# Loading x two groups ahead, counting in a sequence of its own and spreading the offset stores in a four-layer convolution kernel

## The chip, the cores and the metric

The kernel runs on one core of a Trainium2 chip. The metric is the device time of one execution in microseconds (us). A core has five engines that run side by side and wait for each other through semaphores: TensorE (PE; its weight loads are shown apart as PEld), VectorE (DVE), ScalarE (ACT), GpSimd (POOL) and SyncE (SP). SP issues nearly all DMAs of this kernel.

## The reference, cut to what matters

Four layers are applied to `x`, an array of 4 x 128 x 128 x 128 floats (batch, channel or row, row or column, column), each as `x = x + layer(group_norm(x))`. The change lies in the first, a deformable 3x3 convolution with a rectifier:

```python
offset = jnp.einsum('bchw,oc->bohw', x, w_off) + b_off[None, :, None, None]
# py, px: the position of each tap plus its offset; (y0, x0) its floor
val = gather(y0i, x0i) * (wy0 * wx0)[:, :, None]
...
return jnp.einsum('bgckhw,ogck->bohw', val, wg)      # wg: w_def by groups
...
x = x + _L0_conv_ref(_gn(x), L0_conv_w_off, L0_conv_b_off, L0_conv_w_def)
```

For each of 9 taps and 4 groups of channels every pixel has an offset of its own, and the value there is interpolated from four neighbours. The group normalization `_gn` takes its statistics over 4 neighbouring columns, all rows and all of axis 1, in each batch, so they must be known before the batch's offsets can be computed. The other layers are a scan along rows with a 9-tap convolution, a message layer, and a triangle multiplication with gates. They are the same before and after.

## The kernel before, in words

`deform_layer` (line 182) computes the first layer. It doesn't gather. It lays a table of normalized pixels out in DRAM (`tabs`), with 32 windows of 4 columns plus their margins along each row, and stores the offsets in DRAM (`offs`), in three bf16 parts that add up to a float. A batch is cut into 43 blocks of 3 output rows; with 4 batches there are 172. For a block the offsets come back as `places`, the table as `pixels`. TensorE spreads the offsets of a tap over 120 lanes (`spread_offsets`, line 459, into `t_ps`, two buffers), ScalarE makes the distance and a tent of it (`tents`, 471), VectorE the second tent's negative and VectorE or GpSimd, in turn, the product (`product`, 478). `sample` (484) multiplies the pixels with the products, `keep_samples` (498) copies the samples out of PSUM (`v_ps`, two buffers), and `convolved` (540) makes the convolution, with `finish` (516) adding `x` and storing.

The order of instructions on all five engines is written out by hand: each engine executes them in the order in which the program emits them. The main loop (line 652) has eight units per block, one for each group of four windows. In a unit, spreading runs two units ahead, tents one unit ahead, and products are made for the coming block. At the end of a unit `step` is called once, or twice while fewer than 26 rows are ready beyond the block.

`step` (583) advances a generator to its next `yield`. This is the work beside the main loop, one generator at a time: `counted` (326), the statistics of a whole batch from 1 MB loads, four steps of eight statistics instructions for each of the 8 loads and then the normalization; `prepared` (359), which prepares a chunk of 16 rows; or `x1_norm`, for the layer's result. The loads of `counted` and `prepared` share one buffer, `xin`. A chunk in `prepared` has 32 steps: the load of 16 rows (line 364), then for each of 4 groups of 4 rows seven steps: transposes (371), the normalized `rows` on ScalarE with the stores to the table after every second group (374 to 381), the matmul of the offsets (386), their scale and shift, and three steps that split them into `parts` (ScalarE's copy, line 405, with VectorE's running maximum and minimum and GpSimd's subtraction). Last come 18 stores from `parts` to `offs` (line 419), six to a step, and the end. `parts` is one buffer for a chunk of 16 rows.

SP's queue is in order too. At the start of each block it takes the four loads of `places` for the block after next, the four of `pixels` for the next block, and one of the residual `xres`; the loads and stores of `prepared` come between them where they were emitted. `need` (603) makes the steps that a load of `places` requires, if they were not made yet.

Of the kernel before, what the change touches and what calls it, by code (L numbers as in the profile page):

```python
# [2 lines left out]

# [6 lines left out]
F32 = mybir.dt.float32  # L10
# [3 lines left out]
ALU = mybir.AluOpType  # L14
# [4 lines left out]
P = 128  # L19
# [162 lines left out]
def deform_layer(tc, c, small, x, w_off, b_off, w_def, x1, tabs, offs):  # L182
# [13 lines left out]
    with ExitStack() as ctx:  # L196
# [126 lines left out]

        scales = {}

        def counted(b, dense):

            stats = one.tile([P, NGN, S // RC, 6], F32, name="stats0")
            for r in range(S // RC):
                if dense:  # L330
                    xc = three.tile([P, RC, S], F32, name="xc", tag="v")
                else:
                    xc = one.tile([P, RC, S], F32, name="xin")
                nc.sync.dma_start(xc, x[b, :, r * RC : (r + 1) * RC, :])
                yield
                for g in range(NGN):
                    nc.vector.bn_stats(stats[:, g, r, :], xc[:, :, g * GS : (g + 1) * GS])
                    if g % 8 == 7:
                        yield
            got = []  # L340
            yield from gn_steps(nc, c, one, keep, ps_g, stats, "x", got)
            _, s, t = got
            across = ps_g.tile([2 * NL, 2, P], F32, name="st_ps", tag="gn_ps")
            for i, v in enumerate((s, t)):
                diag = one.tile([P, P], F32, name=f"diag_{i}")
                nc.vector.tensor_scalar(diag, c.ident, v, None, ALU.mult)
                nc.tensor.matmul(
                    across[:, i], lhsT=c.ones[:, 0 : 2 * NL], rhs=diag, start=True, stop=True
                )
            yield  # L350
            st = keep.tile([2 * NL, 2, P], F32, name="st")
            nc.vector.tensor_copy(st, across)

            koff = keep.tile([2 * NL, S], F32, name="koff")
            nc.vector.tensor_scalar(koff, st[:, 1], wsum, boff, ALU.mult, ALU.add)
            scales[b] = (s, t, st, koff)
            yield

        def prepared(b, y0):

            s, t, st, koff = scales[b]
            table = tabs[b].rearrange("x (r s) c -> x r s c", s=SX)
            xc = one.tile([P, RC, S], F32, name="xin")
            nc.sync.dma_start(xc, x[b, :, y0 : y0 + RC, :])
            yield
            for h in range(0, RC, RO):
                if h % (2 * RO) == 0:
                    rows = one.tile([P, 2 * RO, P], F32, name="rows")
                pt = ps_g.tile([P, RO, P], F32, name="img_ps", tag="gn_ps")
                for i in range(RO):  # L370
                    nc.tensor.transpose(pt[:, i], xc[:, h + i, :], c.ident)  # L371
# [12 lines left out]
                yield  # L384
                po = ps_g.tile([2 * NL, RO, S], F32, name="off_ps", tag="gn_ps")
                nc.tensor.matmul(po, lhsT=woff, rhs=xc[:, h : h + RO, :], start=True, stop=True)
# [9 lines left out]
                n = (b * S + y0 + h) // RO  # L396
                flat = off.rearrange("p r c -> p (r c)")

                rest = one.tile([2 * NL, RO, S], F32, name="rest")
                left = off  # L400
                for i in range(NSPLIT):
                    part = parts[:, i, h * OW : (h + RO) * OW].rearrange(
                        "p (r c) -> p r c", c=OW
                    )[:, :, 2 : S + 2]
                    nc.scalar.copy(part, left)
                    if i < 2:
                        nc.vector.tensor_reduce(
                            ranges[:, i, n : n + 1], flat, AX.X, (ALU.max, ALU.min)[i]
                        )
                    if i + 1 < NSPLIT:  # L410
                        nc.gpsimd.tensor_tensor(rest, left, part, ALU.subtract)
                        left = rest
                    yield
            for k in range(NK):
                ky, kx = k // 3 - 1, k % 3 - 1
                r0 = (y0 + ky + 1) * OW
                for d in range(2):
                    p0 = d * NL + k * NG
                    nc.sync.dma_start(
                        offs[b][d, k % 2, :, k // 2, r0 : r0 + RC * OW].rearrange(  # L420
                            "(n g) c -> g n c", g=NG
                        ),
                        parts[p0 : p0 + NG, :, 1 - kx : 1 - kx + RC * OW],
                    )
                if k % 3 == 2 and k + 1 < NK:
                    yield

        def load_places(b, j):
            t = places[(b * NYB + j) % 3]
# [39 lines left out]
            return tp, n  # L469

        def tents(tp, n):
            dist = two.tile([LANES, 2, NB], F32, name="dist")
            nc.scalar.activation(dist[:, :, 0:n], tp[0:LANES, :, 0:n], AF.Abs)  # L473
            tent = two.tile([LANES, NB], F32, name="tent")
            nc.scalar.activation(tent[:, 0:n], dist[:, 0, 0:n], AF.Relu, bias=1.0, scale=-1.0)  # L475
            return dist, tent, n

        def product(m, dist, tent, n, engine):

            neg = two.tile([LANES, NB], F32, name="neg")  # L480
            nc.vector.tensor_scalar(neg[:, 0:n], dist[:, 1, 0:n], 1.0, 1.0, ALU.min, ALU.subtract)  # L481
            engine.tensor_tensor(m, neg[:, 0:n], tent[:, 0:n], ALU.mult)  # L482

        def sample(m, pix, i, rows):

# [86 lines left out]
        beside = {"now": None, "norms": [], "count": 1}  # L572
# [6 lines left out]
        def rows_of(b, y0):  # L579
            yield from prepared(b, y0)  # L580
            ready[b] = y0 + RC

        def step(b, row):

            if beside["now"] is None:
                nb = next((i for i in range(b, B) if ready[i] < S), B)
                lead = (nb - b) * S + (ready[nb] if nb < B else 0) - row
                if beside["norms"]:
                    beside["now"] = beside["norms"].pop(0)
                elif beside["count"] <= min(nb, B - 1) or (lead > 20 and beside["count"] == b + 1 < B):  # L590
                    beside["now"] = counted(beside["count"], False)
                    beside["count"] += 1
                elif nb < B:
                    beside["now"] = rows_of(nb, ready[nb])
                else:
                    return False
            try:
                next(beside["now"])
            except StopIteration:
                beside["now"] = None  # L600
            return True

        def need(b, row):
            while ready[b] <= min(row, S - 1):
                step(b, row)

# [35 lines left out]
        for _ in counted(0, True):  # L642
            pass
        load_row(0)
        load_row(1)
# [6 lines left out]
        for n, (b, j) in enumerate(blocks):  # L652
# [11 lines left out]
            for i in range(NG_X):  # L664
# [8 lines left out]
                if end and i < 6:  # L673
# [4 lines left out]
                    else:  # L678
                        product(me[:, kx, :], *tents(*ends[kx]), nc.vector)
                count(6)  # L680
                for _ in range(2 if ready[b] < min(S, RY * j + 26) else 1):
                    step(b, RY * j + 2)
            for _ in convs:
                pass
            if j == 0:
# [22 lines left out]
            pass  # L708
        count(len(to_count))
        beside["norms"].append(x1_norm(B - 1, stats))  # L710
        while step(B, S):
            pass


# [671 lines left out]
```

## Time and profile before

| what | us |
|---|---|
| runs before: lowest, median, highest | 8644.56, 8714.38, 8768.25 |
| the profiled execution | 8805.67 |
| its span, first to last instruction | 8803.9 |
| first sampling matmul (line 491) | 245.7 |
| last copy of samples (line 507) | 4455.9 |
| busy in the span: PE, DVE, ACT, POOL | 7117.6, 5000.0, 3346.5, 1721.0 |

The profile is one execution; the profiled one took 91 us more than the median. Its page gives busy times by engine, 40 slices of the span (about 220 us each), and groups of instructions by line, with the name of the tile written, an arrow, and the tiles read. "Idle before" is the time an engine stood before an instruction, and the releaser is what ended that. A line of the timeline has start, duration, engine, line, operation and, in brackets, the idle time before it; like instructions in a row are merged. SPq is SP's DMA queue: its times are those of issuing a DMA, not of moving the data. The deformable layer lies in the first 20 slices.

### The profile page before, as it was taken

What the parts mean: (1) busy time and instruction counts of PE and PEld (TensorE: products, weight loads), DVE (VectorE), ACT (ScalarE), POOL (GpSimd) and SP (SyncE); (2) the same over time, 40 slices, a digit from 0 to 9 for tenths busy, and PEclk for the clock granted to TensorE, in tenths of its full rate; (3) what the DMA queues carried; (4) which work ended last, traced back from release to release, by engine and by line L of the source; (5) the groups of instructions that cost most, each with busy time, mean ns of one, the idle gap of its engine ahead of it and who ended that gap; (6) DMA issues with size and microseconds to landing.
All of it is one profiled execution on the core that took longest, in us unless ns stands there. A gap on an engine that the chain in (4) does not pass through costs nothing. (4 is left out here: it accounts for less than half of the span.)

```text
span 8803.9 us, 105220 instructions
## 1 busy us (share of the span) xinstructions
PE 7117.6 (81%) x35800; PEld 5835.4 (66%) x35800; DVE 5000.0 (57%) x13104; ACT 3346.5 (38%) x5404; POOL 1721.0 (20%) x1791
## 2 busy tenths in 40 slices
PE   0668777978789777799989999698679668966986
PEld 0556565756567556677778888398549647963985
DVE  5545555755557555577744444447626752674466
ACT  0445554555555555466621111122312312231223
POOL 0123222233222223222200000112112120212121
PEclk9778887988878888799999999688759876976897
DMA  2333333433333333343321221100100010001000
GB/s 66 88 67 77 76 74 69 98 76 80 73 72 98 72 74 76 68 80 61 64 65 60 67 67 54 53 1 10 42 25 1 20 58 1 1 29 48 1 10 29
DMA packets 978744, 473.48 MB, mean 54 GB/s; under 512 B 705076, under 2 KB 931988, under 8 KB 963860
## 3 DMA queue, kind: packets, MB, share of 16 engines
q1 hardware_dynamic: 951216, 428.93, 20.3%
q10 hardware_dynamic: 26980, 37.73, 1.2%
q8 instruction: 284, 4.65, 0.2%
q14 instruction: 264, 2.16, 0.1%
HBM read 284.15 MB, written 182.35 MB: 53 GB/s over the span
## 5 line engine op out<-in xcount | busy, mean ns | idle before, releaser
L491 PEld LDWEIGHTS v_ps<-m,pixels 120*128 120x128 f32 x11008 | 1512.9, 206 | 221.5 <-issue 69.3
L473 ACT ACTIVATE dist<-t_ps 120x780 f32<-120x780 f32 x1560 | 1266.5, 812 | 983.6 <-DVE neg L481 848.5
L491 PE MATMUL v_ps<-m,pixels 120*128 120x108 f32 (+1 forms) x11008 | 1610.0, 291 | 20.1 <-DVE v L502 14.9
L502 DVE COPY v<-v_ps 128x432 f32<-128x432 f32 x1376 | 809.6, 588 | 1390.4 <-PE v_ps L491 1386.9
L551 PE MATMUL conv_ps<-v,wneg 128*128 128x128 f32 (+2 forms) x5160 | 1382.6, 403 | 14.8 <-DVE v L507 14.8
L482 POOL TENSOR_TENSOR m<-neg,tent 120x390 f32<-120x390 f32 x688 | 700.9, 1019 | 2785.1 <-DVE neg L481 2508.1
L551 PEld LDWEIGHTS conv_ps<-v,wneg 128*128 128x128 f32 x5160 | 851.6, 205 | 305.5 <-issue 181.6
L1029 PE MATMUL conv_ps<-carry,wconv 128*128 128x256 f32 x4572 | 1009.5, 378 | 0.3 <-issue 0.3
L1029 PEld LDWEIGHTS conv_ps<-carry,wconv 128*128 128x128 f32 x4572 | 850.8, 188 | 121.3 <-issue 0.6
L475 ACT ACTIVATE tent<-dist 120x390 f32<-120x390 f32 x1560 | 823.0, 528 | 213.7 <-POOL m L482 155.9
L1226 PE MATMUL proj_ps<-wcat,X 128*128 128x128 f32 x4096 | 903.0, 384 | 0.0
L1226 PEld LDWEIGHTS proj_ps<-wcat,X 128*128 128x128 f32 x4096 | 901.5, 313 | 0.0
L1231 DVE SCALAR_TENSOR_TENSOR work<-proj_ps,rstd,pbias 128x128 f32<-128x128 f32 x2048 | 613.2, 344 | 293.3 <-issue 173.7
L464 PE MATMUL t_ps<-places,spread 14*120 14x390 bf16 x3096 | 581.4, 388 | 214.2 <-ACT dist L473 166.1
L482 DVE TENSOR_TENSOR m<-neg,tent 120x390 f32<-120x390 f32 x860 | 652.1, 758 | 91.1 <-DVE neg L481 1.4
L481 DVE TENSOR_SCALAR neg<-dist 120x390 f32<-120x390 f32 x1560 | 630.9, 414 | 42.2 <-ACT dist L473 41.2
L464 PEld LDWEIGHTS <-spread 14*120 14x120 bf16 x3120 | 221.8, 129 | 515.8 <-issue 414.8
L1011 ACT ACTIVATE rowT<-x1T_ps,t_x,s_x 128x128 f32<-128x128 f32 x512 | 192.4, 458 | 862.7 <-PE x1T_ps L1007 417.2
L371 PE MATMUL img_ps<-ident,xin 128*128 128x128 f32 x512 | 98.1, 325 | 514.4 <-DMA xin<-in_x_dram 511.5
L1240 POOL TENSOR_TENSOR right<-work,sig 128x128 f32<-128x128 f32 x512 | 240.6, 471 | 1362.4 <-ACT sig L1236 1138.0
L1303 PE MATMUL gT_ps<-ident,cen 128*128 128x128 f32 x512 | 124.0, 424 | 468.5 <-DVE cen L1298 412.1
L1236 ACT ACTIVATE sig<-work 128x256 f32<-128x256 f32 x512 | 213.4, 417 | 639.1 <-DVE work L1231 639.1
(185 smaller groups left out, 8134.4 us busy)
## 6 DMA issues: line engine op xcount, KB each, us to landing
pixels<-tab SPq DMA_DIRECT2D x688, 120.0 KB
xin<-in_x_dram SPq DMA_DIRECT2D x56, 1024.0 KB
tab<-rows SPq DMA_DIRECT2D x384, 128.0 KB
x<-x1c SPq DMA_DIRECT2D x32, 1024.0 KB
x1rows<-x SPq DMA_DIRECT2D x128, 256.0 KB
x2T<-x2c ACTq DMA_DIRECT2D x128, 256.0 KB
X<-x2T SPq DMA_DIRECT2D x16, 2048.0 KB
out_dram<-res SPq DMA_DIRECT2D x64, 512.0 KB
```

The lines of the kernel that those rows point to most:

```text
L464: nc.tensor.matmul(tp[0:LANES, d, 0:n].rearrange("p (r c) -> p r c", c=PADW), lhsT=spread[p0 : p0 + 14, :], rhs=src[p0 : p0 + 14, k, :, 0: ...
L473: nc.scalar.activation(dist[:, :, 0:n], tp[0:LANES, :, 0:n], AF.Abs)
L475: nc.scalar.activation(tent[:, 0:n], dist[:, 0, 0:n], AF.Relu, bias=1.0, scale=-1.0)
L481: nc.vector.tensor_scalar(neg[:, 0:n], dist[:, 1, 0:n], 1.0, 1.0, ALU.min, ALU.subtract)
L482: engine.tensor_tensor(m, neg[:, 0:n], tent[:, 0:n], ALU.mult)
L491: nc.tensor.matmul(vp[:, h * n : h * n + rows * w].rearrange("p (k c) -> p k c", c=w), lhsT=pix[0:LANES, xb, :], rhs=m[:, :, RX * xb : RX ...
L502: nc.vector.tensor_copy(v[:, :, c0 : c0 + full * RX].rearrange("p k (h c) -> p k h c", c=RX), vp[:, 0 : full * n].rearrange("p (h k c) -> ...
L551: nc.tensor.matmul(pc[:, at : at + r1 - r0, :], lhsT=wneg[:, 3 * ky + kx, :], rhs=v[:, k0 + kx, r0:r1, kx : kx + S], start=m == 0, stop=m ...
L1029: nc.tensor.matmul(pc, lhsT=wt[:, k, :], rhs=old[h][:, :, k : k + S], start=(k == 0), stop=(k == TAPS - 1),)
L1226: nc.tensor.matmul(pp[:, j], lhsT=X[:, :, j0 + j], rhs=wcat[:, cols], start=True, stop=True)
L1231: nc.vector.scalar_tensor_tensor(pre[:, j], pp[:, j], rstd[:, j0 + j : j0 + j + 1], pbias[:, cols], ALU.mult, ALU.add,)
L1240: nc.gpsimd.tensor_tensor(right[:, j0 : j0 + 4, :], pre[:, :, DQ : 2 * DQ], sig[:, :, DQ:], ALU.mult)
```

## The change

It has four parts, all in `deform_layer`.

1. `prepared` takes its rows in loads of 4 rows (256 KB) into three buffers instead of 16 rows into one, and `load_group` issues the loads of the next two groups with each group. The first three are loaded before the first batch is counted. The step that held the load is gone.
2. The statistics of the next batch are no longer one of the generators of `step`. `count_of` loads half rows (16 rows of 64 columns, 512 KB) into a buffer of its own, and the main loop advances it once per unit, from the second unit of a batch on, beside `step`. Each half row takes four units of waiting for the load and two with eight statistics instructions each. After it, `scales_of` is put in line for `step`. Batch 0 is counted at once ahead of the loop.
3. The 18 stores of a chunk's offsets are put on a list when the chunk is done. Three are emitted in each unit, and what is left is emitted in the first group of the next chunk, just ahead of the copies that write `parts` again. A chunk counts as ready when its last store has been emitted. A chunk is now 28 steps and an end.
4. `tents` and `product` keep distance, tent and negative in one tile with three buffers, overwritten in place, instead of three tiles with two buffers each.

The core of the diff:

```diff
-        def counted(b, dense):
+        def count_of(b, stats):
             for r in range(S // RC):
...
+                for h in range(2):
+                    xc = one.tile([P, RC, S // 2], F32, name="xhalf")
+                    nc.sync.dma_start(
+                        xc, x[b, :, r * RC : (r + 1) * RC, h * S // 2 : (h + 1) * S // 2]
+                    )
+                    for _ in range(4):
+                        yield
+                    for g in range(NGN // 2):
+                        nc.vector.bn_stats(
+                            stats[:, h * NGN // 2 + g, r, :], xc[:, :, g * GS : (g + 1) * GS]
+                        )
+                        if g % 8 == 7:
+                            yield
...
+        def load_group(n):
+            if n not in loaded and n < B * S // RO:
+                b, y = n * RO // S, n * RO % S
+                loaded[n] = three.tile([P, RO, S], F32, name="xin")
+                nc.sync.dma_start(loaded[n], x[b, :, y : y + RO, :])
+
+        def store(n):
+            for _ in range(min(n, len(to_store))):
+                to_store.pop(0)()
...
         def prepared(b, y0):
...
-            xc = one.tile([P, RC, S], F32, name="xin")
-            nc.sync.dma_start(xc, x[b, :, y0 : y0 + RC, :])
-            yield
             for h in range(0, RC, RO):
+                n = (b * S + y0 + h) // RO
+                load_group(n)
+                load_group(n + 1)
+                load_group(n + 2)
+                xc = loaded.pop(n)
...
                 yield
+                if h == 0:
+                    store(len(to_store))
                 flat = off.rearrange("p r c -> p (r c)")
...
-            for k in range(NK):
...
-                for d in range(2):
-                    p0 = d * NL + k * NG
-                    nc.sync.dma_start(
...
-                if k % 3 == 2 and k + 1 < NK:
-                    yield
+            def store_tap(k, d):
...
+                nc.sync.dma_start(
...
+                if (k, d) == (NK - 1, 1):
+                    ready[b] = y0 + RC
+            to_store.extend(partial(store_tap, k, d) for k in range(NK) for d in range(2))
...
         def tents(tp, n):
-            dist = two.tile([LANES, 2, NB], F32, name="dist")
-            nc.scalar.activation(dist[:, :, 0:n], tp[0:LANES, :, 0:n], AF.Abs)
-            tent = two.tile([LANES, NB], F32, name="tent")
-            nc.scalar.activation(tent[:, 0:n], dist[:, 0, 0:n], AF.Relu, bias=1.0, scale=-1.0)
-            return dist, tent, n
+            d = three.tile([LANES, 2, NB], F32, name="dist")
+            nc.scalar.activation(d[:, :, 0:n], tp[0:LANES, :, 0:n], AF.Abs)
+            nc.scalar.activation(d[:, 0, 0:n], d[:, 0, 0:n], AF.Relu, bias=1.0, scale=-1.0)
+            return d, n
...
                 count(6)
+                store(3)
                 for _ in range(2 if ready[b] < min(S, RY * j + 26) else 1):
-                    step(b, RY * j + 2)
+                    step()
+                if not (j == 0 and i == 0):
+                    next(beside["count"], None)
+                elif b + 1 < B:
+                    beside["count"] = counting(b + 1)
```

More of the change, by code (lines that the diff above doesn't have):

```diff
@@ L1 @@
 from contextlib import ExitStack
+from functools import partial
 from itertools import chain
@@ L324, in deform_layer, with count_at_once, scales_of @@
         scales = {}
-        def counted(b, dense):
-            stats = one.tile([P, NGN, S // RC, 6], F32, name="stats0")
+        def count_of(b, stats):
             for r in range(S // RC):
-                if dense:
-                    xc = three.tile([P, RC, S], F32, name="xc", tag="v")
-                else:
-                    xc = one.tile([P, RC, S], F32, name="xin")
+                for h in range(2):
[11 more added lines that the diff above has]
+                            yield
+        def count_at_once(b, stats):
+            for r in range(S // RC):
+                xc = three.tile([P, RC, S], F32, name="xc", tag="v")
                 nc.sync.dma_start(xc, x[b, :, r * RC : (r + 1) * RC, :])
-                yield
                 for g in range(NGN):
                     nc.vector.bn_stats(stats[:, g, r, :], xc[:, :, g * GS : (g + 1) * GS])
-                    if g % 8 == 7:
-                        yield
+        def scales_of(b, stats):
             got = []
@@ L357, in counted @@
             yield
+        loaded = {}
+        to_store = []
+        def load_group(n):
[6 more added lines that the diff above has]
+                to_store.pop(0)()
         def prepared(b, y0):
@@ L362, in prepared @@
             table = tabs[b].rearrange("x (r s) c -> x r s c", s=SX)
-            xc = one.tile([P, RC, S], F32, name="xin")
-            nc.sync.dma_start(xc, x[b, :, y0 : y0 + RC, :])
-            yield
             for h in range(0, RC, RO):
+                n = (b * S + y0 + h) // RO
[3 more added lines that the diff above has]
+                xc = loaded.pop(n)
                 if h % (2 * RO) == 0:
@@ L370, in prepared @@
                 for i in range(RO):
-                    nc.tensor.transpose(pt[:, i], xc[:, h + i, :], c.ident)
+                    nc.tensor.transpose(pt[:, i], xc[:, i, :], c.ident)
                 yield
@@ L385, in prepared @@
                 po = ps_g.tile([2 * NL, RO, S], F32, name="off_ps", tag="gn_ps")
-                nc.tensor.matmul(po, lhsT=woff, rhs=xc[:, h : h + RO, :], start=True, stop=True)
+                nc.tensor.matmul(po, lhsT=woff, rhs=xc, start=True, stop=True)
                 yield
@@ L395, in prepared @@
                 yield
-                n = (b * S + y0 + h) // RO
+                if h == 0:
+                    store(len(to_store))
                 flat = off.rearrange("p r c -> p (r c)")
@@ L413, in prepared @@
                     yield
-            for k in range(NK):
+            def store_tap(k, d):
                 ky, kx = k // 3 - 1, k % 3 - 1
                 r0 = (y0 + ky + 1) * OW
-                for d in range(2):
-                    p0 = d * NL + k * NG
[L419 to L424, printed above, removed]
-                if k % 3 == 2 and k + 1 < NK:
-                    yield
+                p0 = d * NL + k * NG
+                nc.sync.dma_start(
+                    offs[b][d, k % 2, :, k // 2, r0 : r0 + RC * OW].rearrange(
+                        "(n g) c -> g n c", g=NG
+                    ),
+                    parts[p0 : p0 + NG, :, 1 - kx : 1 - kx + RC * OW],
+                )
+                if (k, d) == (NK - 1, 1):
+                    ready[b] = y0 + RC
+            to_store.extend(partial(store_tap, k, d) for k in range(NK) for d in range(2))
         def load_places(b, j):
@@ L471, in tents, with product @@
         def tents(tp, n):
-            dist = two.tile([LANES, 2, NB], F32, name="dist")
-            nc.scalar.activation(dist[:, :, 0:n], tp[0:LANES, :, 0:n], AF.Abs)
-            tent = two.tile([LANES, NB], F32, name="tent")
-            nc.scalar.activation(tent[:, 0:n], dist[:, 0, 0:n], AF.Relu, bias=1.0, scale=-1.0)
-            return dist, tent, n
[L478 to L482, printed above, removed]
+            d = three.tile([LANES, 2, NB], F32, name="dist")
+            nc.scalar.activation(d[:, :, 0:n], tp[0:LANES, :, 0:n], AF.Abs)
+            nc.scalar.activation(d[:, 0, 0:n], d[:, 0, 0:n], AF.Relu, bias=1.0, scale=-1.0)
+            return d, n
+        def product(m, d, n, engine):
+            nc.vector.tensor_scalar(
+                d[:, 1, 0:n], d[:, 1, 0:n], 1.0, 1.0, ALU.min, ALU.subtract
+            )
+            engine.tensor_tensor(m, d[:, 1, 0:n], d[:, 0, 0:n], ALU.mult)
         def sample(m, pix, i, rows):
@@ L571, in deform_layer @@
         ready = [0] * B
-        beside = {"now": None, "norms": [], "count": 1}
+        beside = {"now": None, "norms": [], "rows": 0, "count": iter(())}
         def x1_norm(b, stats):
@@ L577, in x1_norm, with counting, step @@
             norms[b] = got[1:]
[L579 to L583, printed above, removed]
+        def counting(b):
+            stats = one.tile([P, NGN, S // RC, 6], F32, name="stats0")
+            yield from count_of(b, stats)
+            beside["norms"].append(scales_of(b, stats))
+        def step():
             if beside["now"] is None:
-                nb = next((i for i in range(b, B) if ready[i] < S), B)
-                lead = (nb - b) * S + (ready[nb] if nb < B else 0) - row
+                b, y0 = divmod(beside["rows"], S)
                 if beside["norms"]:
                     beside["now"] = beside["norms"].pop(0)
[L590 to L594, printed above, removed]
+                elif b < B and b in scales:
+                    beside["now"] = prepared(b, y0)
+                    beside["rows"] += RC
                 else:
@@ L604, in need @@
             while ready[b] <= min(row, S - 1):
-                step(b, row)
+                store(len(to_store))
+                if ready[b] <= min(row, S - 1) and not step():
+                    next(beside["count"], None)
         DONE = [1, 2, 3, 5, 6, 7, 8, 9]
@@ L641, in deform_layer @@
         ctx.enter_context(tc.manual_schedule(engines=order))
-        for _ in counted(0, True):
+        stats = one.tile([P, NGN, S // RC, 6], F32, name="stats0")
+        for n in range(3):
+            load_group(n)
+        count_at_once(0, stats)
+        for _ in scales_of(0, stats):
             pass
@@ L680, in deform_layer @@
                 count(6)
+                store(3)
                 for _ in range(2 if ready[b] < min(S, RY * j + 26) else 1):
-                    step(b, RY * j + 2)
+                    step()
+                if not (j == 0 and i == 0):
+                    next(beside["count"], None)
+                elif b + 1 < B:
+                    beside["count"] = counting(b + 1)
             for _ in convs:
@@ L710, in deform_layer @@
         beside["norms"].append(x1_norm(B - 1, stats))
-        while step(B, S):
+        while step():
             pass
```

## The prediction

> **What bounds the kernel now.** I read first the page's slices and the busy times by stretch, to see where in the span the change can act at all. The slices are tenths of busy time, and the granted TensorE clock, over 220 us each.
>
> ```profile
> PE   0668777978789777799989999698679668966986
> ...
> PEclk9778887988878888799999999688759876976897
> ```
>
> ```profile
> 660.00:1320.00 660.00, 524.63 (x3000) 397.38 (x2999) 379.32 (x853) 360.26 (x563) 196.43 (x181) 0.84 0.35 76
> 1540.00:1760.00 220.00, 200.24 (x1173) 157.48 (x1172) 176.07 (x626) 126.98 (x194) 48.41 (x47) 0.90 0.43 98
> 3960.00:4400.00 440.00, 437.37 (x2864) 349.40 (x2864) 318.28 (x780) 302.32 (x462) 104.86 (x103) 1.00 0.33 62
> ```
>
> The columns are length, busy us (and instructions) of PE, PEld, DVE, ACT, POOL, then clock, DMA share and GB/s. The deformable layer ends near 4458 us; everything later is not touched. Its last stretch, where no rows are prepared any more, has TensorE busy 437 of 440 us at full clock; the first stretch, with preparation, only 525 of 660 at 0.84. So TensorE is the floor, and preparation costs far more than its matmuls. TensorE's waits from 240 to 3860 us (total us, times, longest) and the timelines of the SP queue and of TensorE say how:
>
> ```profile
> PE img_ps L371 <- DMA xin<-in_x_dram: 511.5, 26, 26.0
> PE t_ps L464 <- ACT dist L473: 158.0, 174, 25.7
> ```
>
> ```profile
> 899.65 10.25 SPq L419 DMA_DIRECT2D off<-parts  x8
> 909.95 1.17 SPq L364 DMA_DIRECT2D xin<-in_x_dram  x1
> ...
> 997.30 21.13 SPq L419 DMA_DIRECT2D off<-parts  x18
> 1018.47 1.21 SPq L364 DMA_DIRECT2D xin<-in_x_dram  x1
> ```
>
> ```profile
> 918.86 1.12 PE L371 MATMUL img_ps<-ident,xin 128*128 128x128 f32 x4 [20.07 <-DMA xin<-in_x_dram]
> ...
> 921.43 1.88 PE L491 MATMUL v_ps<-m,pixels 120*128 120x108 f32 x8
> ...
> 937.04 1.04 PE L491 MATMUL v_ps<-m,pixels 120*128 120x108 f32 x8
> ```
>
> Once per chunk of 16 rows SP issues 18 stores of offsets in 21 us, only then the next 1 MB load of x, and TensorE stands 20 us at the transposes of that load. Afterwards eight sampling matmuls take 1.88 us, not 1.04, until about 937. The spacing of line 507, which runs once per block of 3 rows, is the ruler:
>
> ```profile
> 849.15 0.32 DVE L507 COPY v<-v_ps 128x162 f32<-128x162 f32 x1
> ...
> 868.18 0.31 DVE L507 COPY v<-v_ps 128x162 f32<-128x162 f32 x1
> ```
>
> 19.03 us for a block with preparation and no stall; others read the same way are 19.6 to 20, and the block with the stall about 42.5. I take 19.3, so 2.4 us for each of its eight units. Without preparation it is 17.1 us. A chunk of four blocks, 42.5+21.5+19.03+19.6 = 102.6 us, loses 102.6 - 4x19.3 = 25.4 us: 20 us of wait and 5.4 us of slow clock.
>
> **What the Trainium skill says.** "TensorE: Matmul & The Clock Gate", What's actually happening: after an idle window of about 3.4 us the array runs at half clock until it has been busy a while. The trace agrees (1.88 against 1.04 us). "DMA: Bandwidth & Descriptors", Why a DMA increments its semaphore by 16 and not by 1: a copy is spread over the largest number of DMA engines, up to 16, that divides its slowest dimensions. A store here begins with a dimension of 4, so 4 engines; the trace fits: 50 KB in 1.17 us is 43 GB/s, while the 128 KB table stores take 0.61 us, 210 GB/s. "Perfetto Trace Analysis", Tensor Engine Instruction: ScalarE, VectorE and GpSimd are strict FIFO. Nothing passes a waiting instruction on ACT in the stall at 900 to 919 either.
>
> **The change, part by part.**
>
> *Loads two groups ahead.* A group of 4 rows has seven steps, so its load is issued 14 steps, 34 us, before use. The 1 MB load landed 9 us after its issue behind a full queue; 256 KB cannot need 34. The wait of 511 us at line 371 goes, with its clock: 26 x 25.4 = 660 us.
>
> *What is late next.* The stores stay 18 per chunk. In the burst above the first two issues took 0.26 and 0.29 us and the later ones about 1.2: the queue pushes back, so the rate is the DMA engines', and being emitted three per unit doesn't speed it. Nor does it delay them: SP runs ahead of the units, and began storing 0 to 5 us after ScalarE's last copy into `parts` in nearly every chunk. In the DMA packets of the trace the last of the 18 lands about 24.5 us after that copy. `parts` has one buffer: the first copy of the next chunk (line 405) overwrites it and must wait for all 18. Before, it came 41 us later, since four steps (the load and the spread stores) and TensorE's 20 us stall lay between: free. After, a chunk is 28 steps and an end: last copy in step 27, end, then steps 0' to 4', the first copy in the last of these with the forced rest of the stores ahead of it. That is 6 units, 14.4 us. Into the same stretch of SP's queue fall a load of x (0.8) and, as 29 steps drift against 8 units per block, in 6 of 8 chunks a block's places (3.6), pixels (2.3) and residual (0.6): 24.5 + 0.8 + 0.75 x 6.5 = 30.2. ScalarE waits 30.2 - 14.4 = 16 us (11 without a block's start, 17 with).
>
> Queued behind that copy on ScalarE are `dist` and the tents; for them wait VectorE's and GpSimd's products, and TensorE's next spreading, with two buffers of t_ps. TensorE has about a unit and a half (4 us) before it stops. So it loses 12 us and 5 for the clock: 17 us in place of 25.4. Of 31 transitions, one falls in the start and about five have a normalization of 10 to 12 steps between, which is cover enough; 25 x 17 = 430 us. Net of both: -230 us.
>
> *Fewer steps.* 29 for 32 per chunk: preparation covers about ten blocks less, but its matmuls stay, so only the small waits in such blocks go: 19.3 - 17.1 - 1.1 groups x 1.6 us of matmuls = 0.4, ten blocks, 4 us. Nothing.
>
> *Counting in its own sequence.* 256 instructions of line 337 per batch at 0.21 us are unchanged (54 us x 3). They had units to themselves, in steps of 1.7 us, and the counting blocks in the second stretch above were 20 to 25 us long: about 5 us over the no-preparation floor, 7 blocks, 3 batches, 105 us. After: 96 units, 12 blocks per batch, beside preparation. VectorE then has 379/660 x 25.7 = 14.7 us per block from the first stretch plus 2.7 bursts x 1.7 = 4.5: 19.2 of 19.3. Full; I price it at 2 us per block, 36 blocks, 72 us. Bounds: 0, and 5 us per block, 180. Net -33 us. The half-row loads have 2048 packets of 256 B: nearest rows, half of a 1 MB load issued every 3.3 us (1.7) and the pixels' 960 packets in 0.57 us (1.2); value 1.6, nobody waits if it lands in the four units given.
>
> *The tents' third buffer, in place.* `dist` waits for the product three back instead of VectorE's `neg` two back; instructions and shapes are equal. The micro-waits of TensorE for `dist` are 158 us; I give half of what isn't one 26 us case: -60; bounds -130 and +30, since an odd product is GpSimd's.
>
> *Start.* At two steps per unit the copy comes after 3 units, so the first chunks stall about as today: 0. First loads go ahead of the counting: 0 to -10.
>
> **Sum.** -660 + 430 - 33 - 60, and +20 for double-rate chunks that still lose 24: -303, about -300. The profiled execution took 8805.67 us (span 8803.9), so 8505 for its like; it lies 91 us above the runs' median, which gives 8714 - 300 = 8415.
>
> **Rivals.**
> 1. *The wait for the stores is hidden* (ScalarE far enough ahead, or stores landing sooner beside a less full queue). For it: no wait of ScalarE on a store is in the trace. Against: 24.5 us against 14.4. Then 430 falls to about 0 to 80: 8714 - 700 = 8010.
> 2. *The stall only changes its name.* If ScalarE's 17 us pass to TensorE in full, with 8 us of slow clock, a chunk loses 25 again: 25 x 25 = 625 in place of 430, so 8610. For: the stall of today is the same burst of stores. Against: t_ps and v_ps have two buffers each, which TensorE works off first.
> 3. *Slower: VectorE before late half-row loads.* The half rows for the counting pass through the same SP queue; behind a burst of stores one lands up to 15 us after the units given to it. VectorE, in order, then stops before its statistics, and behind them stand the copies that empty v_ps and the products, so TensorE stops too. My sum has 72 us for 48 half rows, 1.5 us each; the gain of 300 is used up at 1.5 + 300/48 = 7.8 us each. At 9 us the sum is 48 x 7.5 = 360 higher: 8775. For: VectorE is full there, and every half row waits for VectorE to free its only buffer. Against: bursts cover 24 of 70 us of a chunk, so two of three half rows meet none.
>
> **Chances.** Forecast 0.57, rival 1 0.16, rival 2 0.16, rival 3 0.11. The likeliest case alone: 8290 to 8560. The range leaves out rival 3 and part of rival 1: 8000 to 8720. About 2% is what a measurement of this kernel tells from no change. Over 2% faster (below 8540): 0.48 of the forecast's 0.57 and all of rival 1, 0.64; within 2%: 0.29; slower by more: 0.07.
>
> **What would show it.** Right: line 371 waits for no load; ScalarE's copy into `parts` waits for DMA some 25 times, 11 to 17 us each; TensorE waits for `dist` instead, clock dips once per chunk of 3.6 blocks; counting blocks near 21 us. Wrong: blocks of 19 us throughout (rival 1), dips of 20 us (rival 2), statistics waiting for `xhalf` (rival 3). The forecast fails most easily if the six units or the 4 us of TensorE's lead are misjudged.

## The result and the profile after

The changed kernel took 8313.11 us (median of 4 runs, 8228.58 to 8386.98) where the kernel before took 8680.03 (4 runs): a ratio of 0.953, with a 95% interval of 0.9408 to 0.9653. The ratio is taken from fast runs alone, without the one of 8386.98, so it is not the quotient of these medians (0.958), and the profile of before, 8805.67 us, is that of a slow run. The changed kernel's profiled execution has a span of 8322.9 us; that of before had 8803.9.

Not all of these 481 us belong to the change. The copy into `ve`, one of the last in the deformable layer, serves as a ruler, in the view of one tile (line, engine, durations in ns, first and last start in us), first before, then after:

```profile
L507 DVE COPY ve<-v_ps x4: 166/167/167, 1491.6 to 4455.9; 128x18 f32<-128x18 f32 x4
```

```profile
L539 DVE COPY ve<-v_ps x4: 167/167/167, 1342.4 to 4074.8; 128x18 f32<-128x18 f32 x4
```

The last of these copies ends at 4075.0 us, before at 4456.1: in these two profiles the layer became 381 us shorter. The unchanged rest of the kernel took 4247.9 us in this profile and 4347.9 in that of before, so 100 us of the difference of spans lie outside the code that was changed. Even without them the profile of before lies some 26 us above the median of its runs, so 381 us is an upper value, and about 355 an estimate from these numbers. Below, "layer end" is the end of this last copy in a run's profile, one profile for each kernel. It is the sharper ruler, since the rest alone ranged from 4200 to 4303 us over the profiles of the changed kernels, while the two profiles of one kernel, the changed one, have layer ends 11 us apart.

The slices of the page, the same two rows as the prediction shows of before:

```profile
PE   0589888888799788999899998796689569867986
...
PEclk9789888999889898999899999797669769975887
```

There are fewer slices of low clock, but they are still there. The waits say why. TensorE's from 230 to 4100 us (total us, times, longest):

```profile
PE t_ps L496 <- ACT dist L505: 448.0, 89, 21.1
PE t_ps L496 <- DMA places<-off: 52.3, 3, 33.5
PE conv_ps L583 <- DVE v L539: 32.9, 6, 10.1
```

and ScalarE's at the copies into `parts`, before (240 to 4460 us) and after (240 to 4100 us):

```profile
ACT parts L405 <- DMA places<-off: 3.3, 3, 1.9
```

```profile
ACT parts L435 <- DMA xin<-in_x_dram: 273.6, 15, 26.2
ACT parts L435 <- DMA places<-off: 145.6, 10, 20.1
...
ACT parts L435 <- DMA off<-parts: 71.4, 4, 19.1
```

The wait of TensorE for a load of x, 511.5 us before, is gone altogether. In its place ScalarE waits at its copy into `parts` 29 times, 490.6 us together, and TensorE then waits for ScalarE's `dist`. The copy waits for all eight completion counters (semaphores) that the stores use, and later DMAs use the same ones in turn; that is why the view names a load of `xin` or `places` as the releaser of what is a wait for the stores. The DMA packets of the trace confirm it: in 26 of the transitions the copy stands 11.7 us or more, and in each of them it starts 0.4 to 0.9 us after the last packet of the 18 stores has landed. One transition in the timelines of SP, ScalarE and TensorE:

```profile
748.74 1.87 SPq L449 DMA_DIRECT2D off<-parts  x3
750.71 1.47 SPq L380 DMA_DIRECT2D xin<-in_x_dram  x1
752.23 3.69 SPq L464 DMA_DIRECT2D places<-off  x4
756.02 2.18 SPq L482 DMA_DIRECT2D pixels<-tab  x4
758.30 0.70 SPq L577 DMA_DIRECT2D xres<-in_x_dram  x1
759.04 17.63 SPq L449 DMA_DIRECT2D off<-parts  x15
```

```profile
748.10 0.62 ACT L435 CAST parts<-rest 72x512 bf16<-72x512 f32 x1 [0.53 <-POOL rest L441]
780.19 0.62 ACT L435 CAST parts<-off 72x512 bf16<-72x512 f32 x1 [19.62 <-DMA xin<-in_x_dram]
```

```profile
781.58 0.58 PE L496 MATMUL t_ps<-places,spread 14*120 14x390 bf16 x2 [16.05 <-ACT dist L505]
...
783.10 1.88 PE L523 MATMUL v_ps<-m,pixels 120*128 120x108 f32 x8
...
798.47 1.04 PE L523 MATMUL v_ps<-m,pixels 120*128 120x108 f32 x8
```

ScalarE ends the chunk's last copy at 748.7 and SP starts the stores at once. After three of them a load of x and a block's nine loads pass, 8 us, then fifteen stores in 17.6 us. The next copy into `parts` stands 19.6 us; TensorE stands 16.05, less by its lead of 3.6 us, and then needs 1.88 us and more for eight sampling matmuls, until about 795. Over the 26 transitions ScalarE stands 18.8 us on average and TensorE 16.5, so the lead is 2.2 us as a rule.

### The profile page after: what moved, and what is told of

The parts are those of the page before. It is cut to its first block, busy times and chain, and to the rows that moved or that the text cites. A ratio compares the mean times of both kernels' runs of the same rounds, so it can differ in the third digit from the quotient of the medians.

```text
span 8322.9 us, 102555 instructions
## 1 busy us (share of the span) xinstructions
PE 6844.8 (82%) x35800; PEld 5653.5 (68%) x35800; DVE 4928.4 (59%) x13104; ACT 3343.6 (40%) x5404; POOL 1623.0 (20%) x1791
## 4 chain that ended last, share of the span: by engine, by line
PE 39%; DVE 5%; ACT 2%; POOL 2%; issue 1%; DMA 1%; POOLq 0%; ACTq 0%; DVEq 0%; SPq 0%
PE conv_ps L1070 12%; PE proj_ps L1267 11%; PE gate_ps L1321 3%; PE tri_ps L1287 3%; PE out_ps L1350 3%; DVE cen L1339 2%; PE cent_ps L1244 2%; PE out_ps L1349 2%; POOL X L1219 2%; PE var_ps L1250 2%; PE gT_ps L1344 1%; DVE work L1216 1%; DVE gate L1327 1%; ACT L1331 1%; PE x1T_ps L1048 1%
## 5 line engine op out<-in xcount | busy, mean ns | idle before, releaser
L523 PEld LDWEIGHTS v_ps<-m,pixels 120*128 120x128 f32 x11008 | 1458.1, 200 | 207.3 <-issue 54.1
L523 PE MATMUL v_ps<-m,pixels 120*128 120x108 f32 (+1 forms) x11008 | 1556.7, 285 | 18.6 <-DVE v L534 15.1
L583 PE MATMUL conv_ps<-v,wneg 128*128 128x128 f32 (+2 forms) x5160 | 1340.2, 394 | 32.9 <-DVE v L539 32.9
L514 POOL TENSOR_TENSOR m<-dist 120x390 f32<-120x390 f32 x688 | 607.6, 883 | 2041.1 <-DVE dist L511 1836.5
L496 PE MATMUL t_ps<-places,spread 14*120 14x390 bf16 x3096 | 551.0, 383 | 501.1 <-ACT dist L505 448.0
L506 ACT ACTIVATE dist<-dist 120x390 f32<-120x390 f32 x1560 | 823.2, 528 | 49.3
L511 DVE TENSOR_SCALAR dist<-dist 120x390 f32<-120x390 f32 x1560 | 624.2, 410 | 295.3 <-ACT dist L505 294.2
L496 PEld LDWEIGHTS <-spread 14*120 14x120 bf16 x3120 | 194.6, 127 | 772.4 <-issue 669.3
L514 DVE TENSOR_TENSOR m<-dist 120x390 f32<-120x390 f32 x860 | 590.4, 687 | 91.7 <-DVE dist L511 0.9
L1219 POOL TENSOR_TENSOR X<-X,work 128x512 f32<-128x512 f32 x128 | 161.8, 1264 | 1428.1 <-DVE work L1216 1413.0
```

The costliest lines, as they stand in the source:

```text
L496: nc.tensor.matmul(tp[0:LANES, d, 0:n].rearrange("p (r c) -> p r c", c=PADW), lhsT=spread[p0 : p0 + 14, :], rhs=src[p0 : p0 + 14, k, :, 0: ...
L506: nc.scalar.activation(d[:, 0, 0:n], d[:, 0, 0:n], AF.Relu, bias=1.0, scale=-1.0)
L511: nc.vector.tensor_scalar(d[:, 1, 0:n], d[:, 1, 0:n], 1.0, 1.0, ALU.min, ALU.subtract)
L514: engine.tensor_tensor(m, d[:, 1, 0:n], d[:, 0, 0:n], ALU.mult)
L523: nc.tensor.matmul(vp[:, h * n : h * n + rows * w].rearrange("p (k c) -> p k c", c=w), lhsT=pix[0:LANES, xb, :], rhs=m[:, :, RX * xb : RX ...
L583: nc.tensor.matmul(pc[:, at : at + r1 - r0, :], lhsT=wneg[:, 3 * ky + kx, :], rhs=v[:, k0 + kx, r0:r1, kx : kx + S], start=m == 0, stop=m ...
```

## The experiments

All ratios are to the kernel before, run beside each kernel on the same chip. The changed kernel was run again beside one of them. The last column adds up ScalarE's waits for a DMA at its copies into `parts`.

| kernel | median us | ratio, 95% interval | layer end us | ScalarE at `parts` for DMA, us |
|---|---|---|---|---|
| changed kernel | 8313.11 | 0.953 (0.9408 to 0.9653) | 4075.0 | 490.6 |
| changed kernel again | 8333.82 | 0.9591 (0.9538 to 0.9644) | 4085.8 | 494.5 |
| two half buffers | 7780.36 | 0.8952 (0.8864 to 0.904) | 3534.1 | 3.3 |
| half buffers, stores at once | 7820.15 | 0.8992 (0.8946 to 0.9039) | 3575.2 | 3.3 |
| eight empty steps | 7970.65 | 0.921 (0.9117 to 0.9304) | 3724.2 | 94.7 |
| three empty steps | 8170.35 | 0.9393 (0.9317 to 0.9469) | 3946.7 | 342.8 |
| stores at once | 8199.75 | 0.9462 (0.9374 to 0.955) | 3976.0 | 334.0 |
| two buffers of `dist` | 8651.45 | 0.9947 (0.9914 to 0.9979) | 4389.9 | 418.2 |
| the same, loads in the step | 8602.09 | 0.9882 (0.9828 to 0.9936) | 4352.5 | 170.2 |
| counting in the step | 8463.48 | 0.9716 (0.9643 to 0.979) | 4216.3 | 502.9 |
| old tents | 8451.81 | 0.9728 (0.9673 to 0.9783) | 4204.8 | 463.8 |

### Is it the one buffer of parts?

The first kernel gives the split offsets two buffers of 8 rows, in nearly the space of the one of 16:

```diff
-        parts = wp.tile([2 * NL, NSPLIT, RC * OW + 4], BF16, name="parts")
+        halves = [wp.tile([2 * NL, NSPLIT, RH * OW + 4], BF16, name=f"parts_{i}") for i in range(2)]
...
-            for h in range(0, RC, RO):
+            parts = halves[y0 // RH % 2]
+            for h in range(0, RH, RO):
...
-                    beside["rows"] += RC
+                    beside["rows"] += RH
```

> The split offsets get two buffers of 8 rows in place of one of 16, so a copy into one waits for stores that were emitted half a chunk earlier; there are twice as many stores of half the bytes, and two more steps per 16 rows. Theory (the new wait is the write into the one buffer of parts, about 28 transitions of 19 us): ScalarE's copies wait for no DMA, TensorE's blocks are 19 to 20 us throughout, 7750 to 7900 us. Rival (SP's queue and the four DMA engines of the stores are the limit, and the stall moves to late places, pixels or statistics): TensorE waits for places or ScalarE for DMA about as long as now, 8150 to 8400.

It took 7780.36 us. Its waits at `parts` for a DMA (ScalarE, 240 to 3600 us) and its first line of TensorE's waits:

```profile
ACT parts L438 <- DMA off<-parts: 1.7, 2, 1.2
...
ACT parts L438 <- DMA pixels<-tab: 1.1, 1, 1.1
...
ACT parts L438 <- DMA xres<-in_x_dram: 0.5, 1, 0.5
```

```profile
PE t_ps L499 <- ACT dist L508: 46.5, 72, 5.0
PE conv_ps L586 <- DVE v L542: 15.0, 4, 5.1
```

490 us of waiting are 3, TensorE's wait for `dist` falls from 448 to 46.5, and the layer ends 541 us earlier than with one buffer, although SP now issues 36 stores per 16 rows. No other wait of TensorE took its place. The rival, that SP's queue or the DMA engines limit the layer, is refuted. In the trace's record of the clock, which begins near 260 us, TensorE has 191 us of the layer at half clock, against 780 in the changed kernel and 1189 in the profile of before. Its time at full clock hardly differs: 3082, 3041 and 3014 us. So nearly all that the layer gained is time at half clock, the standing still included.

The second and third kernel add no buffer. They only put time between the two copies, as empty steps, eight here and three in the third kernel:

```diff
                 if h == 0:
+                    for _ in range(8):
+                        yield
                     store(len(to_store))
```

> Eight empty steps stand in the first group of a chunk ahead of the forced stores and the first copy into parts, 14 units between the last copy of a chunk and the first of the next instead of 6. No buffer is added and no instruction removed. Theory: 14 units are 33 us, more than the 25 to 31 us of the stores, so the wait goes as with two buffers: 7750 to 7900. Rival (queue or DMA engines are the limit): 8150 to 8400.

> Three empty steps in the same place, a half dose: 9 units, 21 us, between the two copies. Theory: each transition's wait is shorter by 3 x 2.4 = 7 us[...]: 200 to 280 us less, 8030 to 8110. Rival: no dose, 8250 to 8400.

They took 7970.65 and 8170.35 us. More time between the copies means less waiting: 0, 3 and 8 steps give 491, 343 and 95 us of waiting and layers that end at 4075, 3947 and 3724. But both times lie above the expected ranges. Three steps took 148 us from the sum of the waits, 5 us for each of the 29, and not 7 (25 waits of 13.7 us are left, where there were 29 of 16.9). Eight steps end 190 us after the half buffers. Of this 95 us is waiting that is left, the longest 17.9 us. The record of the clock shows where the rest lies: 406 us of this layer are at half clock and 191 with half buffers, while the time at full clock is about the same (3065 and 3082 us). The slow clock that follows each wait that is left is one candidate. Another is that 37 steps per chunk make the preparation last longer: only 27 blocks end after the last copy into `parts`, and not 44, and the chunks are nearer their due time, where two steps are made per unit and the distance in time halves. Neither was tested by itself.

### What does each part of the change do?

*Spreading undone.* The stores are emitted together when the chunk ends:

```diff
-            to_store.extend(partial(store_tap, k, d) for k in range(NK) for d in range(2))
+            for k in range(NK):
+                for d in range(2):
+                    store_tap(k, d)
```

> The spreading alone undone: the 18 stores are emitted together when the chunk ends; everything else is as in the changed kernel. Theory (SP runs ahead, and the stores move at the rate of their DMA engines whatever the order): no difference beyond 60 us, 8250 to 8370, the same wait at the copy into parts. Rival (spreading keeps the queue free for places and pixels): TensorE waits for them too, 8450 or more.

8199.75 us, better than either expectation: the layer ends 99 us earlier than with spreading. The medians differ by 113 us, though the intervals of the ratios overlap. Its waits at the copy (240 to 4000 us):

```profile
ACT parts L435 <- DMA xin<-in_x_dram: 183.7, 15, 18.3
ACT parts L435 <- DMA off<-parts: 87.0, 7, 14.6
ACT parts L435 <- DMA places<-off: 63.3, 5, 14.9
```

27 waits of 12.4 us on average, for 29 of 16.9. The instructions on SP's queue show why. Together, the last store is issued 21.3 us after the chunk's last copy in the median chunk, and the next copy comes 25.4 us after it. Spread, these are 27.8 and 31.7 us: the loads of x, and where a block begins its places, pixels and residual, stand between the stores in the queue. Spreading does not relieve the queue; it lets 6.5 us of loads go ahead of stores on which ScalarE waits.

With half buffers, where nobody waits for the stores, it should not matter:

> Two half buffers of parts, and all 18 stores emitted together when a half chunk ends. Theory (spreading lets the loads of a block fall into the burst and only lengthens the wait at parts; with that wait gone it is neutral): 7740 to 7830 and no wait of a copy for a DMA. Rival (unspread, the burst delays places and pixels): 7850 or more, with TensorE waiting for them.

7820.15 us, the layer ends at 3575, and copies wait only 3.3 us for a DMA, in two waits. The median is 40 us above that of the spread form, but inside the range of that form's own four runs (7730 to 7834 us), so no difference is shown.

*The third buffer undone.* The tile of distance and tent stays in place but has two buffers:

```diff
-            d = three.tile([LANES, 2, NB], F32, name="dist")
+            d = two.tile([LANES, 2, NB], F32, name="dist")
```

> The third buffer alone undone: distance and tents stay in place in one tile, with two buffers. Theory (the small waits of TensorE for dist were worth some 60 us, and the third buffer is what shortens them): the layer ends 0 to 60 us later, 8310 to 8390. Rival (it does nothing, or the wait for GpSimd's product takes back what it gives): within 20 us of the changed kernel.

8651.45 us, a miss by a wide margin: the layer ends 315 us later than in the changed kernel. ScalarE's waits (240 to 4400 us):

```profile
ACT dist L505 <- POOL m L514: 880.4, 529, 7.6
ACT dist L505 <- DVE m L514: 336.7, 335, 11.6
```

In the changed kernel these two were 296.7 and 38.2 us. Working in place means that the buffer comes free only with the product, where before it came free with VectorE's `neg`. With two buffers this makes ScalarE wait for the product of two taps ago; the third pays for the place saved. A loss on every block fits this: among the last twenty blocks before the final, shorter one, where nothing is prepared any more, the median block takes 18.9 us and not 17.0, and 1.9 us on 172 blocks is 327. So this kernel undoes half of an edit, not the edit.

*Loads ahead undone*, on top of that form, for room:

```diff
+            xall = one.tile([P, RC, S], F32, name="xin")
+            nc.sync.dma_start(xall, x[b, :, y0 : y0 + RC, :])
+            yield
             for h in range(0, RC, RO):
                 n = (b * S + y0 + h) // RO
-                load_group(n)
-                load_group(n + 1)
-                load_group(n + 2)
-                xc = loaded.pop(n)
+                xc = xall[:, h : h + RO, :]
```

> The loads ahead undone, on the two-buffer form of the run before for room: 16 rows in one load at the start of the chunk, one step before its transposes, as in the kernel before; spread stores, counting in its own sequence. Theory A (loads ahead were needed, the stall of 20 us at the transposes comes back and covers the wait at parts): 8480 to 8600. Theory B (with spreading only three stores stand ahead of the load on SP's queue, so the load waits 3 to 6 us at TensorE and the copy into parts about 10): 8250 to 8420, and line of the transposes waits under 8 us each.

8602.09 us. The absolute numbers of both theories are void, as they took the two-buffer form for nearly equal to the changed kernel. Against its own base, 8651.45 and a layer end of 4389.9, it is not slower: 4352.5. TensorE's wait at the transposes is back, but short (240 to 4400 us):

```profile
PE t_ps L496 <- ACT dist L505: 416.9, 425, 15.5
PE img_ps L400 <- DMA xin<-in_x_dram: 158.1, 28, 12.2
```

28 waits of 5.6 us, where the kernel before had 26 of 19.7. On SP's queue three stores and not eighteen now stand just ahead of nearly every load. In exchange ScalarE's wait at `parts` fell from 418 to 170 us. So in this form the loads ahead gain nothing beyond what the order of the stores gives: the time is lost at one place or at the other. This is the second theory's mechanism, though some waits passed its 8 us. Whether it holds with three buffers of `dist` too, where ScalarE waits far less for the products (335 us, not 1217), was not tried.

*Counting sequence undone.* The counting goes back into the one sequence of `step`, after a chunk (the main part of the edit):

```diff
-                if not (j == 0 and i == 0):
-                    next(beside["count"], None)
-                elif b + 1 < B:
-                    beside["count"] = counting(b + 1)
+                if j == 1 and i == 0 and b + 1 < B:
+                    beside["norms"].append(counting(b + 1))
```

with one step, not four units, between a load and its statistics.

> The counting sequence undone: the half-row loads and statistics of the next batch are made inside the one sequence of step, between two chunks, with one step between load and statistics. Theory (its own sequence was priced at a gain of 33 us): 8280 to 8420, preparation ends later, statistics wait for their loads. Rival (VectorE beside preparation costs more than the pause of preparation): faster than the changed kernel, below 8250.

8463.48 us, 43 above the expected range; the layer ends 141 us later than in the changed kernel. VectorE waits for the loads (240 to 4300 us):

```profile
DVE stats L337 <- DMA xhalf<-in_x_dram: 102.6, 42, 12.5
```

11.1 us, once, in the changed kernel. The long blocks (over 28 us, by the spacing of the copy at the end of each block) are 36 instead of 32, and hold 88 us more. These two are of the size of the loss; they may overlap, and I have not separated them. Nor is this form quite the old one: before, the statistics waited 67.3 us in 17 times for their 1 MB loads, here 102.6 in 42 for half rows. So 141 us need not be what the sequence alone is worth.

*Old tents.* Three tiles with two buffers each, as before. For 2 KB of room the counting loads quarter rows, with two units of waiting, so that its length stays:

```diff
-            d = three.tile([LANES, 2, NB], F32, name="dist")
...
+            dist = two.tile([LANES, 2, NB], F32, name="dist")
...
+            tent = two.tile([LANES, NB], F32, name="tent")
...
+            neg = two.tile([LANES, NB], F32, name="neg")
...
-                    xc = one.tile([P, RC, S // 2], F32, name="xhalf")
+                    xc = one.tile([P, RC, S // 4], F32, name="xhalf")
```

> The tents' part alone undone as far as it fits: distance, tent and negative in three tiles with two buffers each, as in the kernel before. For the 2 KB that this takes, the counting loads quarter rows instead of half rows, twice as many, with two units of waiting instead of four, so its length in units stays. The rest is as in the changed kernel. Theory (by the sums so far, 185 us of the layer's 381 came from the exchanged stalls and about 140 from the counting sequence, which leaves some 55 for the tents): 30 to 90 us slower than the changed kernel, 8340 to 8410. Rival (in place costs nothing and the third buffer does not matter against the old form): within 25 us.

8451.81 us, above the expected 8340 to 8410, beside 8333.82 for the changed kernel run with it:

> The changed kernel itself again, beside the run before on the same chip: about 8313, its layer ends near 4075 us.

The layer ends 119 us later. VectorE's statistics wait 61 us for their loads, for 11 in the changed kernel, so up to 50 us may be the quarter rows'. That leaves 70 to 120 us. Among the same last twenty blocks, where nothing is prepared or counted, the old tents cost only 0.2 us a block (17.20 us on average against 16.99), which would be 36 us over 172 blocks. So I put the tents at 36 to 120 us, an estimate; how much of the upper part is theirs stays open.

## Why the prediction was right

*The time.* The forecast was 300 us less; the medians differ by 367 and the layer by up to 381. (A fourth run of before, 8645.69 us, brought its median from 8714.38 to 8680.03, so 300 us less stands for 8380 and not for 8415.) The mechanism is the forecast one, but that the total is so near is partly luck. The terms missed in both directions: the exchange of one stall for the other gained less than forecast, counting and probably the tents more.

*What is late next.* This is the step that the forecast stood on, and it held: ScalarE's copy waits for the stores, TensorE stops after it, and half clock follows. The half buffers show that this wait is the cause. Its size was under-priced, at the two places that the forecast itself had named. The stores released the copy nearly when expected, 31.3 us after the last copy (median of the 26 long waits) for 30.2. But the six units before it passed in 12.6 us and not 14.4, so ScalarE waited 18.8 us for 16, and TensorE's lead was 2.2 us and not 4, so it stood 16.5 us where the sum had 12. The blocks over 28 us, but for the three at the ends of batches, are 29 and hold 534 us beyond 19.3 each, 18.4 us apiece, where 25 of 17 us, 430, were forecast. Over all blocks over 28 us the excess fell from 780 to 595 us, by 185, where the sum had 230 less 20.

*Loads two groups ahead.* Line 371's wait went to nothing, as forecast. That it was the loads that did it is only half the story: with the spread order TensorE waits 5.6 us and no longer 20 for a load in the step (in the form with two buffers of `dist`).

*The spreading.* The step said that spreading neither speeds the stores nor delays them. The first holds; the second was wrong in its wording but not in the sum, which let 5.7 us of loads fall between the stores. The measured 6.5 us per chunk are the price of spreading, some 99 us of the layer, and without that part the change would by this measure have been better.

*Counting.* The term of 33 us was mis-sized: undoing it costs 141 in the form that was run. VectorE beside preparation was bearable, as priced (most blocks took 18 to 23 us while counting). What the sum left out may be the cover of the loads, four units for one step, or the place that the counting took in the sequence; the run changes both.

*The tents.* 60 us were forecast and 36 to 120 are left by the runs. The bound of +30 for GpSimd's late product did not apply with three buffers; with two the layer ended 315 us later. The parts as measured, 185, 141 and 36 to 120, add up to 362 to 446 us for a layer that gained 381 at most: they agree roughly, and they need not be independent.

*The rivals.* Rival 1, the hidden wait, is what the half buffers make true: 8010 was forecast for it and 7780 measured. The under-priced terms of counting and tents are a likely reason, not a separated one. Rival 2 is half true: of ScalarE's 18.8 us TensorE lost 16.5, nearly in full, but such a block lost 18.4 us in all and not 25. Rival 3 did not happen: VectorE waited once, 11.1 us, for a half row.

## What to carry to other kernels

When a wait is taken away, look for the next instruction that the same slow transfers hold back: here the stores that had delayed a load went on to hold their own source buffer. Count the program's steps between that buffer's last use and its next write. Here, spreading the stores over a queue in fixed order didn't thin them out; it let others ahead of them, which helped a load and harmed a store whose buffer was needed. Halving that one buffer into two, on top of this change and at almost no memory, gained another 533 us (8313.11 to 7780.36), more than the 367 of its four parts together. By itself it was not tried, and in the kernel before it would have had only 3.5 us of such waits to remove: a step like this pays once it has become the next thing that is late. And a forecast can come out right in total while its terms do not; only runs that undo one part at a time show it.

## What was not expected of the hardware

Twice as many stores of half the size cost SP's queue nothing. 18 stores of 16 rows, emitted together, are issued in 21.2 us (median), and 18 of 8 rows, emitted together, in 9.4: less than half. And the half clock outlasts the stall. After the stall that ends at 781.58 the record of the clock shows half speed until 796.2, 14.6 us more, and after the stall of before that ended at 918.86 until 935.9, 17.0 us more, though TensorE is busy all the while. Why it takes so long is not shown.
